# One more fill step between a chunk's layer norm and its transposes

## The chip, the cores and the metric

The kernel runs on one core of one Trainium2 chip. The metric is the device time of one execution in microseconds (us), as a median over runs. A core has five engines with queues of their own: PE (TensorE, matmuls and transposes; its weight loads appear as PEld), DVE (VectorE), ACT (ScalarE), POOL (GpSimd) and SP (SyncE, which here issues most DMAs). All data is fp32.

## The reference

The input x is a batch of two images of 128 channels and 64 x 64 places. Two layers are computed:

```
x = x + L0(group_norm(x))               # neighbourhood attention 7x7, 4 heads, and two small MLP steps
t = tokens of x                          # (2, 4096, 128)
q = layernorm(t)
t = t + softmax(q q^T / sqrt(128), diagonal masked) q
u = layernorm(t)
t = t + STU(u)                           # spectral filters (long causal convolutions, 16 of them, and
                                         # their sign-alternated twins), and a short part with 3 lags
out = tokens back to images
```

STU is summed over four branches with a one-hot weight, so that one branch counts. The layer norm of the line `u = layernorm(t)` and what turns u into the two inputs of STU are what the change touches.

## The kernel before, in words

**Stages.** Layer 0 runs first for both images, in an order written out by hand, up to about 350 us. Then come the attention of image 0, the attention of image 1, and the spectral convolution of both images with the output. The attention of image 0 covers leftovers of layer 0 and the preparation of image 1; the attention of image 1 covers leftovers of image 0 and the preparation of the filter matrices.

**Attention.** `attention(b, fill)` (L881) splits the 4096 tokens of image b into 8 chunks of 512, taken in the order CHUNKS = 0, 1, 4, 5, 2, 3, 6, 7. The scores are symmetric, so only the 36 pairs (a, c) with c at or after a are computed. A pair has four slots, numbered 0 to 3. In a slot PE computes the scores of a block of 128 tokens for the *next* pair (`weights`, L898, two half matmuls), ACT takes their exponential (L905), and PE applies the current pair's exponentials to the values: on a diagonal pair onto `own` (L926), else onto `other` (L951). On an off-diagonal pair, after slots 1 and 3, `turned` transposes blocks of exponentials (L912), DVE copies and sums them (L915), and one slot later they go onto `own` as well (L926). When a chunk has had its last contribution, `onto` calls `fill(CHUNKS[a], part)`, which puts a generator `after(b, c, part)` into the list `urgent`. This falls at the start of the next diagonal pair, in its slot 0. The last pair, (7, 7), has no next one, and so no `weights`.

**Filling.** At the end of each slot the loop calls `fill()` (L956), which advances one generator by one step: the first of `urgent` if there is one, else the first of `steps`. A generator that ends is dropped and the next one is asked. For image 0, `steps` holds the leftovers of layer 0 (`drain`), the branch weights, the filters' transform (`filters`, L1156) and the token norms of image 1 (`tokens`). For image 1 it holds what was left of image 0's `urgent` list, then `filter_matrices` (loads `st`, DVE sums L1107 to L1125) and `load_blocks`. `filler` (L1181) makes the pair of `fill` and `urgent`.

**After a chunk.** The steps of `after` (L968) are: transpose the chunk's attention output back to tokens (PE, L975) and divide and add the residual (DVE, L977 to L980); the layer norm into z (`layernorm`, L986: DVE statistics L170 and L171, DVE L160, POOL power L161, DVE L178); transpose z (PE, L989, which goes through the helper `transposed` and so shows as L189) and copy it to `zc` (ACT, L991); three steps with the segment transform of z (PE, L1011 twice and L1019), each with copies to `ub` (DVE and ACT, three buffers) and stores to `us` in HBM on SP's queue (L1000). After the fourth and the eighth chunk `short_lags` is appended, with eight steps (transposes of tt, L189 as well, and blocks of six half matmuls with `zc`, L1043, summed on DVE, L1050).

**The end of image 1.** The first `short_lags` of image 1 is kept back in `kept`. What is left in `urgent` after the attention of image 1 is run with one step of `kept` for each yield (L1259 to L1261). Then the convolution starts; its first loads (`ut`, L1287) reuse memory of image 1's tokens tt and read what was stored to `us`.

**Order.** PSUM banks for all this come from a ring of six (`bank`). In these stages the order in which the code emits instructions is a priority; the framework may place an instruction that is ready ahead of one emitted earlier on the same engine. In the convolution PE's order is the written one.

Of the kernel before, what the change touches and what calls it, by code (L numbers as in the profile page):

```python
# [93 lines left out]
def kernel(  # L94
# [87 lines left out]
    def layernorm(dst, src):  # L182

        ln_apply(dst, src, ln_statistics(src))

    def transposed(ps, src):

        for j in range(src.shape[1]):
            nc.tensor.transpose(ps[:, j * P : (j + 1) * P], src[:, j, :], ident)  # L189
# [667 lines left out]
    with ap_:  # L857
# [6 lines left out]
        def bank():  # L864
            return ps_m.tile([P, 512], F32, tag="bank", name="bank")
# [102 lines left out]
        def after(b, c, part):  # L968

            n0 = 4 * c  # L970
            ph, f0 = divmod(n0, FB)
            par, h = divmod(ph, 2)
            pt = bank()
            for j in range(4):
                nc.tensor.transpose(pt[:, j * P : (j + 1) * P], xa[b][:, (n0 + j) * P : (n0 + j + 1) * P], ident)  # L975
            rden = sp.tile([P, 4], F32, tag="rden", name="rden")
            nc.vector.tensor_reduce(rden, part[:, n0 : n0 + 4, :], AX.X, ALU.add)  # L977
            nc.vector.reciprocal(rden, rden)
            for j in range(4):
                nc.vector.scalar_tensor_tensor(  # L980
                    tt[b][:, n0 + j, :], pt[:, j * P : (j + 1) * P], rden[:, j : j + 1], tt[b][:, n0 + j, :],
                    ALU.mult, ALU.add,
                )
            yield
            z = sp.tile([P, 4, P], F32, tag="z4", name="z4")
            layernorm(z, tt[b][:, n0 : n0 + 4, :])  # L986
            yield
            pt = bank()
            transposed(pt, z)  # L989
            s0 = 1 + h * (TH // 2)  # L990
            nc.scalar.copy(  # L991
                zc[:, par, s0 : s0 + TH // 2].rearrange("p (c f) -> p f c", f=FB)[:, f0 : f0 + 4, :],
                pt.rearrange("p (f c) -> p f c", f=4),
            )
            yield
            z2 = z.rearrange("p f d -> p (f d)")

            def store(m0, q, src):
                mn = min(P, NC - m0)
                nc.sync.dma_start(  # L1000
                    out=us[m0 // 2 : (m0 + mn) // 2, :, 2 * h + q, f0 : f0 + 4, b, par, :].rearrange(
                        "g r f d -> (g r) f d"
                    ),
                    in_=src.rearrange("p (f d) -> p f d", d=P),
                )

            for m0 in (0, P):
                for q in range(2):
                    rows_ = slice(q * SB, (q + 1) * SB)
                    pu = bank()  # L1010
                    nc.tensor.matmul(pu, lhsT=tr[rows_, h, m0 : m0 + P], rhs=z2[rows_], start=True, stop=True)  # L1011
                    ub = sp.tile([P, 512], F32, tag="ub", name="ub", bufs=3)
                    (nc.scalar.copy if q else nc.vector.tensor_copy)(ub, pu)
                    store(m0, q, ub)
                yield
            pu = bank()
            for q in range(2):
                rows_ = slice(q * SB, (q + 1) * SB)
                nc.tensor.matmul(pu[rows_], lhsT=tr[rows_, h, 2 * P : NC], rhs=z2[rows_], start=True, stop=True)  # L1019
            ub = sp.tile([P, 512], F32, tag="ub", name="ub", bufs=3)  # L1020
            nc.scalar.copy(ub, pu)
            for q in range(2):
                store(2 * P, q, ub[q * SB : (q + 1) * SB])
            yield

        def short_lags(b, h):


            for par in range(2):
                n0 = (par * 2 + h) * FB  # L1030
                for f0 in range(0, FB, 4):
                    pt = bank()
                    transposed(pt, tt[b][:, n0 + f0 : n0 + f0 + 4, :])
                    nc.scalar.copy(xa[b][:, (n0 + f0) * P : (n0 + f0 + 4) * P], pt)
                    yield
                xv = xa[b][:, n0 * P : (n0 + FB) * P].rearrange("p (f c) -> p f c", f=FB)
                for c0 in range(0, P, 64):
                    py = bank()
                    for lag in range(3):
                        from_par = (par - lag) % 2  # L1040
                        back = (lag - par + from_par) // 2
                        s0 = 1 + (h * P + c0) * FB - back
                        nc.tensor.matmul(  # L1043
                            py, lhsT=mu[:, lag, :], rhs=zc[:, from_par, s0 : s0 + 512], start=(lag == 0), stop=(lag == 2)
                        )
                    pv = py.rearrange("p (c f) -> p f c", f=FB)
                    first = h == 0 and c0 == 0
                    for lo, hi, s in ((0, 32, 0), (32, 64, 1)) if first else ((0, 64, 2 + h),):
                        xs = xv[:, :, c0 + lo : c0 + hi]
                        nc.vector.scalar_tensor_tensor(  # L1050
                            xs, pv[:, :, lo:hi], seg[:, s : s + 1], xs, ALU.mult, ALU.add
                        )
                    yield
# [127 lines left out]
        def filler(b, steps, kept=None):  # L1181

            urgent, done = [], []

            def fill(c=None, part=None):
                if c is not None:
                    done.append(c)
                    urgent.append(after(b, c, part))
                    if len(done) % 4 == 0:
                        held = kept if kept is not None and len(done) == 4 else urgent  # L1190
                        held.append(short_lags(b, len(done) // 4 - 1))
                    return
                for queue in (urgent, steps):
                    while queue:
                        if next(queue[0], 0) is None:
                            return
                        queue.pop(0)

            return fill, urgent
# [294 lines left out]
```

## Time and profile before

| | |
|---|---|
| median of 3 runs | 2233.68 us (2232.13 to 2233.82) |
| the profiled execution | 2235.26 us |
| its span, first to last instruction | 2233.6 us |
| busy in the span: PE, PEld, DVE, ACT, POOL | 2165.4, 1333.8, 932.9, 783.4, 276.7 us |
| granted TensorE clock, mean | 0.991 |
| PE busy from 460 to 850 us | 383.58 of 390 |
| PE busy from 850 to 916 us | 62.08 of 66 |
| PE busy from 916 to 960 us | 44.00 of 44 |
| PE busy from 960 to 1290 us | 325.16 of 330 |
| PE busy from 1290 to 1330 us | 37.01 of 40 |

A row of the profile has a start, a duration, an engine, a line of the code, the operation with what it writes and reads, and how many instructions of that kind follow each other. A bracket at its end tells how long the engine stood idle before it and what released it. Matmuls are pipelined: they overlap on PE, so the distance between starts says more than durations. The five stretches of the table are the attention of image 0 from its first finished chunk, the first slots of image 1 with the leftovers of image 0, a stretch with attention alone, the rest of image 1, and the end of image 1 up to the convolution.

### The profile page before, as it was taken

The page shows a single profiled execution, that of the slowest core. Times are in us where ns is not written, and L with a number is a line of the kernel's source. Part 1 is how long each engine was busy: PE and PEld are TensorE (multiplying, and loading weights), DVE is VectorE, ACT ScalarE, POOL GpSimd, SP SyncE. Part 2 cuts the span into 40 slices and gives each one's busy share as a digit, 9 for nine tenths or more (in the row PEclk, how much of TensorE's full clock was granted, in tenths as well). Part 3 has the DMA queues.
Part 4 walks back from the last instruction along what each step waited for, and adds up shares of the span by engine and source line. Part 5 has one row for each costly group of instructions (what it writes and reads, how often), then busy time and mean ns, then how long its engine had stood idle before and what let it go on. Part 6 is the DMA issues. An engine that isn't in the chain of part 4 may idle for free.

```text
span 2233.6 us, 31536 instructions
## 1 busy us (share of the span) xinstructions
PE 2165.4 (97%) x11856; PEld 1333.8 (60%) x11856; DVE 932.9 (42%) x3038; ACT 783.4 (35%) x1904; POOL 276.7 (12%) x353
## 2 busy tenths in 40 slices
PE   5899998999999999999999999999999999999998
PEld 3577774544454444544544447677677777777766
DVE  4799985434443346433333342222213232323232
ACT  2789983222332223222222332322323232222232
POOL 3367874200000000000000000000000000000000
PEclk8999998999999999999999999999999999999999
DMA  4222222011000016100000122222222121212101
GB/s 110 72 62 61 61 55 51 1 57 62 24 24 22 8 44 181 38 24 15 10 24 24 47 82 68 50 48 59 47 51 59 39 59 39 59 39 59 40 10 76
DMA packets 174810, 109.53 MB, mean 49 GB/s; under 512 B 26049, under 2 KB 159809, under 8 KB 174146
## 3 DMA queue, kind: packets, MB, share of 16 engines
q1 hardware_dynamic: 171818, 105.24, 18.0%
q10 hardware_dynamic: 2840, 2.27, 0.4%
q8 instruction: 94, 1.54, 0.3%
q14 instruction: 58, 0.48, 0.1%
HBM read 72.87 MB, written 34.60 MB: 48 GB/s over the span
## 4 chain that ended last, share of the span: by engine, by line
PE 86%; DVE 6%; POOL 3%; DMA 2%; ACT 1%; issue 1%; SPq 1%; ACTq 0%; POOLq 0%; DVEq 0%
PE acc L1318 25%; PE pc L1306 13%; PE bank L898 10%; PE own L926 10%; PE other L951 8%; PE bank L912 4%; PE bank L332 2%; PE bank L189 2%; PE bank L542 2%; PE bank L1011 1%; PE bank L1043 1%; PE py L1340 1%; DMA st<-in_m_minus_dram 1%; PE po L564 1%; PE bank L506 1%
## 5 line engine op out<-in xcount | busy, mean ns | idle before, releaser
L1307 DVE COPY y<-pc 128x512 f32<-128x512 f32 x320 | 221.6, 692 | 351.5 <-PE pc L1306 347.8
L905 ACT ACTIVATE e<-bank 128x512 f32<-128x512 f32 x288 | 171.9, 597 | 552.5 <-PE bank L898 417.3
L898 PE MATMUL bank<-cm 128*128 128x512 f32 x576 | 298.9, 603 | 1.4 <-DVE y L653 1.4
L1318 PE MATMUL acc<-y,mpl 128*128 128x256 f32 x1280 | 292.1, 382 | 0.0
L1318 PE MATMUL acc<-y,mmi 128*128 128x256 f32 x1280 | 288.0, 379 | 0.0
L1306 PE MATMUL pc<-ct,ut 64*128 64x512 f32 x1280 | 285.2, 595 | 0.9 <-issue 0.9
L1318 PEld LDWEIGHTS acc<-y,mpl 128*128 128x128 f32 x1280 | 238.1, 190 | 59.4 <-issue 29.6
L1318 PEld LDWEIGHTS acc<-y,mmi 128*128 128x128 f32 x1280 | 242.6, 190 | 32.7
L1307 ACT COPY y<-pc 128x512 f32<-128x512 f32 x320 | 205.0, 641 | 86.5 <-PE pc L1306 86.5
L951 PE MATMUL other<-e,tok 128*128 128x512 f32 x448 | 228.6, 592 | 0.0
L926 PE MATMUL own<-et,tok 128*128 128x512 f32 x448 | 227.1, 594 | 1.4 <-DVE part L915 1.4
L915 DVE CUSTOM_DVE_ANT_0 et<-bank,one 128x512 f32<-128x512 f32 x224 | 145.7, 688 | 166.5 <-PE bank L912 166.3
L1306 PEld LDWEIGHTS pc<-ct,ut 64*128 64x128 f32 x1280 | 121.5, 187 | 145.8 <-issue 140.6
L1325 ACT COPY ob<-acc 128x256 f32<-128x256 f32 x32 | 19.3, 604 | 387.0 <-PE acc L1318 387.0
L926 PEld LDWEIGHTS own<-et,tok 128*128 128x128 f32 x448 | 84.4, 190 | 109.7 <-issue 72.6
L951 PEld LDWEIGHTS other<-e,tok 128*128 128x128 f32 x448 | 85.0, 190 | 106.6 <-issue 105.9
L898 PEld LDWEIGHTS bank<-cm 128*128 128x128 f32 x576 | 95.7, 193 | 73.8 <-issue 44.7
L1342 DVE TENSOR_TENSOR xa<-py,xa 128x512 f32<-128x512 f32 x32 | 22.1, 692 | 281.4 <-PE py L1340 281.4
L912 PEld LDWEIGHTS bank<-ident,e 128*128 128x128 f32 x896 | 103.3, 142 | 57.2 <-issue 43.6
L161 POOL TENSOR_TENSOR ln_rs<-ln_rs,mhalf 128x4 f32<-128x4 f32 x24 | 24.3, 1012 | 847.6 <-DVE ln_rs L160 847.6
L529 ACT ACTIVATE p<-p,mn 128x196 f32<-128x196 f32 x256 | 114.4, 449 | 22.2 <-DVE mn L519 14.0
L912 PE MATMUL bank<-ident,e 128*128 128x128 f32 x896 | 117.6, 274 | 0.0
(208 smaller groups left out, 2292.4 us busy)
## 6 DMA issues: line engine op xcount, KB each, us to landing
ut<-us SPq DMA_DIRECT2D x80, 256.0 KB
us<-ub SPq DMA_DIRECT2D x64, 256.0 KB
vw<-vd SPq DMA_DIRECT2D x256, 49.0 KB
ct<-gs SPq DMA_DIRECT2D x160, 72.0 KB
ct<-gs SPq DMA_DIRECT2D x160, 64.0 KB
gs<-sum SPq DMA_DIRECT2D x20, 256.0 KB
vd<-v SPq DMA_DIRECT2D x128, 32.0 KB
st<-in_m_plus_dram SPq DMA_DIRECT2D x16, 256.0 KB
```

The lines of the kernel that those rows point to most:

```text
L189: nc.tensor.transpose(ps[:, j * P : (j + 1) * P], src[:, j, :], ident)
L332: nc.tensor.matmul(pl, lhsT=wg[:, lo : lo + P], rhs=zT, start=True, stop=True)
L529: nc.scalar.activation(p, p, AF.Exp, bias=t[name + "mn"][:, h : h + 1], scale=-1.0, accum_out=t["den"][:, u, h : h + 1],)
L898: nc.tensor.matmul(ps, lhsT=cm[b][:, n * P : (n + 1) * P], rhs=cm[b][:, chunk(c)], start=True, stop=True)
L905: nc.scalar.activation(e, ps, AF.Exp, bias=0.0, scale=ASCALE, accum_out=part[:, n, c : c + 1])
L912: nc.tensor.transpose(pt[:, k * P : (k + 1) * P], es[k][:, m * P : (m + 1) * P], ident)
L915: nc.vector.tensor_tensor_reduce(et, pt, one, 1.0, 0.0, ALU.mult, ALU.add, part[:, n, a : a + 1])
L926: nc.tensor.matmul(own, lhsT=tok[b][:, n, :], rhs=e, start=first, stop=last)
L951: nc.tensor.matmul(other, lhsT=tok[b][:, 4 * CHUNKS[a] + j, :], rhs=es[j], start=(j == 0), stop=(j == 3))
L1306: nc.tensor.matmul(pc, lhsT=ut[fp, b, par, :], rhs=cv_[fp], start=True, stop=True)
L1307: (nc.scalar.copy if f else nc.vector.tensor_copy)(y[:, 4 * f : 4 * f + 4, :, par, b * 2 * FB + q : (b + 1) * 2 * FB : 2], pc.rearrange("p ...
L1318: nc.tensor.matmul(acc, lhsT=(mmi if l else mpl)[:, k, :], rhs=y[:, 1::2, k, ::-1, :] if l else y[:, 0::2, k, :, :], start=(l == 0 and k = ...
```

## The change

`after` yields twice between the norm and the transposes of z: once as before (None), and once with the value True. `fill` gives a True a meaning of its own: the generator has used its turn without work, so `fill` leaves the first list and takes a step of the next list, `steps`, if there is one. The generator stays where it is, and goes on with the transposes at the next call. A generator's end is now told by False instead of 0. Where `after` runs as part of `steps` (the leftovers of image 0 during image 1), the True ends the call without work; in the loop after the attention of image 1 it takes one more step of `kept`.

```diff
             z = sp.tile([P, 4, P], F32, tag="z4", name="z4")
             layernorm(z, tt[b][:, n0 : n0 + 4, :])
             yield
+            yield True
             pt = bank()
             transposed(pt, z)
             s0 = 1 + h * (TH // 2)
```

```diff
                         held.append(short_lags(b, len(done) // 4 - 1))
                     return
+
                 for queue in (urgent, steps):
                     while queue:
-                        if next(queue[0], 0) is None:
+                        got = next(queue[0], False)
+                        if got is None:
                             return
+                        if got:
+                            break
                         queue.pop(0)
```

## The prediction

> **What bounds the kernel now.** I read the page first. TensorE (PE) is busy for 97% of the span, and the chain that ended last is 86% PE. So an edit pays only where it removes time in which PE stands still, and it costs only where it makes PE stand still.
>
> ```profile
> PE 2165.4 (97%) x11856; PEld 1333.8 (60%) x11856; DVE 932.9 (42%) x3038; ACT 783.4 (35%) x1904; POOL 276.7 (12%) x353
> ```
>
> Next I read the view of waits for PE alone: engine and waiting line, what it waited for, total us, times, longest. Its first row is the step that the diff touches: the transposes of z (written at L189) wait for the norm's last instruction (L178).
>
> ```profile
> PE bank L189 <- DVE z L178: 14.5, 14, 3.2
> ```
>
> Then I looked at one of the fourteen in the order of PE's time (start, duration, line, what it writes and reads). L975 transposes the chunk, then come the norm's other engines, then z's transposes; L898 and L926 are attention.
>
> ```profile
> 709.75 0.60 PE L975 MATMUL bank<-ident,xa 128*128 128x128 f32 x4
> 710.18 1.02 PE L898 MATMUL bank<-cm 128*128 128x512 f32 x2
> 711.04 1.02 PE L926 MATMUL own<-e,tok 128*128 128x512 f32 x2
> 711.90 1.02 PE L898 MATMUL bank<-cm 128*128 128x512 f32 x2
> 712.76 1.02 PE L926 MATMUL own<-e,tok 128*128 128x512 f32 x2
> 714.52 0.75 PE L189 MATMUL bank<-ident,z 128*128 128x128 f32 x3 [0.74 <-DVE z L178]
> 715.11 1.02 PE L898 MATMUL bank<-cm 128*128 128x512 f32 x2
> 715.97 0.27 PE L189 MATMUL bank<-ident,z 128*128 128x128 f32 x1
> ```
>
> Starts tell more than the bracket. An attention pair starts every 0.86 us, so z could start at 712.76 + 0.86 = 713.62. It starts at 714.52, 0.90 late. Then the first three transposes come one by one as DVE delivers: L898 follows after 0.59 where four transposes otherwise take 0.43 (709.75 to 710.18). By the next transform (L1011 at 717.03) PE is behind an unbroken row (713.62 + 0.43 + 2 x 0.86 + 0.09 = 715.86) by 1.17 us. I use 1.17, not 0.74. The norm behind it, on DVE, with its one step on POOL (1.01 us, L161):
>
> ```profile
> 710.38 1.12 DVE L980 SCALAR_TENSOR_TENSOR tt<-bank,rden,tt 128x128 f32<-128x128 f32 x4 [1.66 <-PE bank L975]
> 712.67 0.17 DVE L160 TENSOR_SCALAR ln_rs<-ln_mv 128x4 f32<-128x4 f32 x1
> 714.03 1.11 DVE L178 TENSOR_SCALAR z<-tt,ln_mv,ln_rs 128x128 f32<-128x128 f32 x4 [1.19 <-POOL ln_rs L161]
> ```
>
> From L975's start to z's first transpose are 4.77 us; PE has 0.43 + 4 x 0.86 = 3.87 us of other work there. Eleven stalls have this shape (0.68 to 0.75): chunks 0, 1, 5, 2, 3 of image 0 and 0, 1, 4, 5, 2, 3 of image 1. Chunk 4 of image 0 shows no wait of PE itself, but starts slip by some 0.6. The others are two 1.60 stalls (chunk 6 of each image) and one of 3.21:
>
> ```profile
> 836.97 1.00 PE L189 MATMUL bank<-ident,z 128*128 128x128 f32 x4 [1.60 <-DVE z L178]
> 858.22 1.10 PE L189 MATMUL bank<-ident,z 128*128 128x128 f32 x4 [3.21 <-DVE z L178]
> ```
>
> [...] halves of 0.59 us start every 0.43. Hence the starts above. [...] at the 3.21 stall: DVE's filter sums wait for a load while the chunk's L980, whose transposes were issued at 850.11, stands behind them.
>
> ```profile
> 851.27 0.75 DVE L1109 SCALAR_TENSOR_TENSOR mmi<-st,wt,mmi 128x512 f32<-128x512 f32 x1 [1.07 <-DMA st<-in_m_minus_dram]
> 853.91 1.12 DVE L980 SCALAR_TENSOR_TENSOR tt<-bank,rden,tt 128x128 f32<-128x128 f32 x4
> ```
>
> **The change part by part.** No instruction is added or removed. A fill slot is one call of fill() in the attention loop. Now the slot after the norm belongs to `steps`, and z's transposes and the chunk's three transform steps come one slot later, with their stores (six DMAs a chunk, on SP's queue).
>
> 1. The extra slot as cover. Counting by the code, L975 falls in slot 0 of a diagonal pair's four, the norm in slot 1, the transposes in slot 2 before and 3 after: one more L898 and L926, 1.72 us. `steps` adds work only for chunks 0, 1, 4 of image 0 (filter sums, token norms) and chunk 0 of image 1 (a load); elsewhere it is empty, and attention alone is the cover. 3.87 + 1.72 = 5.59 us against 4.77: 0.8 to spare. All eleven go: 11 x 1.17 = 12.9 us. Chunk 4 of image 0: 0.6. Bounds by the bracket and by starts: 8.1 and 12.9; I take starts.
>
> 2. Chunk 6 of both images: its diagonal pair is the last, has no L898, and `steps` is empty. PE already runs all three remaining L926 pairs ahead of z (2.74 us from 832.63), so one slot later is the same place. 0.
>
> 3. Chunk 7 of image 0 runs in image 1's first slots, as part of `steps`. L975 comes one slot later (1.72), and between it and z there is 0.43 + 7 x 0.86 + 0.87 (eight transposes L912) = 7.3 us instead of 4.7. If DVE still begins L980 at 853.9, z comes at 858.2, that is 6.4 after the new L975: covered. By starts the stall cost 3.38 and about 0.7 behind it, 4.1 in all. But what is late next is known: from 838 to 911 the chain that ended last goes through the loads of the filter matrices, and PE's waits for L915 at 892.64 (0.56) and 911.14 (0.15) are bound by them through DVE's queue. PE arriving earlier waits longer there, unless those loads move up too. Bounds 0 and 4.1; I take 1.5.
>
> 4. The end of image 1. What is left after attention is mixed with the held short lags, one of theirs per yield. Before, chunk 7's norm lies under two short-lag blocks:
>
> ```profile
> 1301.42 0.60 PE L975 MATMUL bank<-ident,xa 128*128 128x128 f32 x4
> 1301.85 5.32 PE L1043 MATMUL bank<-zc,mu 128*128 128x512 f32 x12
> 1307.01 0.60 PE L189 MATMUL bank<-ident,z 128*128 128x128 f32 x4
> ```
>
> Chunk 6 leaves one step more, which uses up one short-lag block; chunk 7 then has L975, one block (2.58), two sets of transposes (0.43 each), z: 0.43 + 2.58 + 0.86 = 3.87 against 4.77. A new stall of 0.9 by the bracket's kind, 1.3 by starts; I take -1.1. Its stores come some 3 us later. Before, the transforms end at 1314.46 and SP has passed its stores by 1318.3; the first conv load is released at 1324.2 by the last tt transposes, not by stores. After, there lie 0.86 + 5.16 + 0.86 = 6.9 us from the last transform to the end of these transposes, and the stores need 3.9. Hidden, with 3.0 to spare; were that gone, each us would delay the conv stage by one.
>
> ```profile
> 1324.27 2.24 SPq L1287 DMA_DIRECT2D ut<-us  x5
> ```
>
> 5. The queues that the moved steps pass. The middle transform now comes directly ahead of L912, whose sums on DVE (L915) release L926. The DVE copy (0.69) can begin after half of the transform, before L912's first half is done: hidden; without that cover 0.69 per chunk. A store that holds up the next ub copy on ACT delays an exp that PE wants a pair later. Together with 838 to 911 I allow 1.4 for waits that I can't place (0 to 6).
>
> Sum: 12.9 + 0.6 + 0 + 1.5 - 1.1 - 1.4 = 12.5. The profiled execution took 2235.26 (span 2233.6 and 1.7 around it), 1.6 above the median shown: 2222.8 for such an execution, 2233.68 - 12.5 = 2221.2 for the median. I write 2221.5.
>
> **Rivals.** B: given back in part. The later transforms crowd the off-diagonal pairs, where L915's sums must be on time; 12 chunks x 0.69 = 8.3 back: about -5, 2229. For: 33.8 us of idle time ahead of L926's weight loads ends on L915's sums. Against: the loads overlap matmuls, and outside 838 to 911 PE waited for L915 only twice, 0.35 each.
>
> C: slower. DVE's queue between 838 and 911 holds 20.6 us of waits for the filter loads, most of them hidden now. If the changed order puts L915's sums behind them, PE pays. It decides above 12.4 us of that (12.9 + 0.6 - 1.1 is gained elsewhere), and is slower by a measurable amount above 16.9; all 20.6 would give +8, 2242. For: 3.21 us of such a wait already reached PE at 858. Against: since then they cost PE only 0.71.
>
> D: the change doesn't do what it says. The written order is a priority and instructions are placed by readiness (one L898 stands ahead of z's last transpose now). If z kept its place: 2233.7. Against: the added L898 and L926 now come ahead in the written order and wait for nothing new.
>
> **How the numbers follow.** The main case 0.70, B 0.14, C 0.09, D 0.07. The main case's own range is 2217 to 2226 (all of item 3: 2218.6, without the allowance a little less; the bracket's 8.1 in place of 12.9: 2226). To reach 8 in 10 I add most of B: 2215 to 2230. About 0.2%, 4.5 us, is what a measurement can tell from no change: faster 0.70 + 0.12 of B = 0.82; same 0.02 of B and 0.06 of D = 0.08; slower 0.10.
>
> **What would show it.** Right: the wait of L189 for z falls from 14.5 to about 4 (two 1.60, one new near the end of image 1); in the chunk shown, three L898 and three L926 between L975 and four z transposes in a row; PE's busy time unchanged; the conv stage starts some 12 us earlier, the same length. Wrong: PE's waits for L915 growing by more than 3 us; a conv start bound by us stores; chunk 6 losing its 1.60, which would make it better than I say.

## The result and the profile after

| | before | after |
|---|---|---|
| median | 2234.49 us (2232.13 to 2237.20) | 2224.14 us (2222.13 to 2226.11) |
| the profiled execution | 2235.26 us, span 2233.6 | 2222.13 us, span 2220.4 |
| first transposes (L975) of image 0's first chunk | 470.64 | 470.75 |
| first matmul of the convolution | 1330.24 | 1317.11 |
| from there to the end of the span | 903.3 | 903.3 |

After over before is 0.9951, 95% interval [0.9940, 0.9962]: faster by 10.3 us, or 0.5%. The predicted time was 2221.5 us, 2.6 us less, with a range of 2215 to 2230. Between the two profiled executions it is 13.13 us, all of it between the first two rows of times.

Lines after L988 have moved by one, those of the convolution by five: the segment transforms are L1012 and L1020 now, the short lags L1044 (PE) and L1051 (DVE), the filter sums L1108 to L1126. PE's line of the page:

```profile
PE 2159.5 (97%) x11856; PEld 1333.2 (60%) x11856; DVE 930.8 (42%) x3038; ACT 783.8 (35%) x1904; POOL 276.8 (12%) x353
```

The instructions are as many as before. In the view of PE's waits (total us, times, longest) the row that held 14.5 us in 14 stalls has three left, and a row that held 1.4 us has grown:

```profile
PE bank L189 <- DVE z L178: 5.0, 3, 2.0
PE own L926 <- DVE part L915: 4.2, 4, 2.9
```

The longest of the second row lies where the 3.21 for z was, in the first slots of image 1:

```profile
854.63 1.12 PE L926 MATMUL own<-et,tok 128*128 128x512 f32 x2 [2.90 <-DVE part L915]
```

PE's order in time, at the chunk that the prediction showed:

```profile
706.97 0.60 PE L975 MATMUL bank<-ident,xa 128*128 128x128 f32 x4
707.41 1.02 PE L898 MATMUL bank<-cm 128*128 128x512 f32 x2
708.27 1.02 PE L926 MATMUL own<-e,tok 128*128 128x512 f32 x2
709.12 1.02 PE L898 MATMUL bank<-cm 128*128 128x512 f32 x2
709.98 1.02 PE L926 MATMUL own<-e,tok 128*128 128x512 f32 x2
710.84 1.02 PE L898 MATMUL bank<-cm 128*128 128x512 f32 x2
711.70 1.02 PE L926 MATMUL own<-e,tok 128*128 128x512 f32 x2
712.56 0.60 PE L189 MATMUL bank<-ident,z 128*128 128x128 f32 x4
```

Three L898 and three L926 instead of two, no bracket, and four transposes of z in one row: from L975 to z are 5.59 us, each of them filled.

The distance between the L975 of successive chunks says what each step brought. Chunks are in their order 0, 1, 4, 5, 2, 3, 6, 7.

| part of the span | before minus after, us |
|---|---|
| the eleven chunks with stalls of 0.68 to 0.75 | 12.75 (1.10 to 1.18 each) |
| chunk 4 of image 0 | 0.62 |
| chunk 6 of image 0 to chunk 0 of image 1 (with chunk 7 of image 0) | 2.22 (130.03 to 127.81) |
| chunk 6 of image 1 to the convolution | -2.35 (38.54 to 40.89) |
| sum | 13.24; the start was 0.11 later: 13.13 |

### The profile page after: what moved, and what is told of

Same layout as the page of the kernel before. It is cut to its first block, busy times and chain, and to the rows that moved or that the text cites. A ratio compares the mean times of both kernels' runs of the same rounds, so it can differ in the third digit from the quotient of the medians.

```text
span 2220.4 us, 31534 instructions
## 1 busy us (share of the span) xinstructions
PE 2159.5 (97%) x11856; PEld 1333.2 (60%) x11856; DVE 930.8 (42%) x3038; ACT 783.8 (35%) x1904; POOL 276.8 (12%) x353
## 4 chain that ended last, share of the span: by engine, by line
PE 88%; DVE 4%; POOL 3%; DMA 2%; SPq 1%; ACT 1%; issue 1%; POOLq 0%; ACTq 0%; DVEq 0%
PE acc L1323 25%; PE pc L1311 13%; PE bank L898 11%; PE own L926 11%; PE other L951 8%; PE bank L912 4%; PE bank L332 2%; PE bank L1044 2%; PE bank L189 1%; PE bank L1012 1%; PE bank L542 1%; PE py L1345 1%; PE po L564 1%; PE bank L506 1%; ACT p L529 1%; POOL tok L703 1%
## 5 line engine op out<-in xcount | busy, mean ns | idle before, releaser
L898 PE MATMUL bank<-cm 128*128 128x512 f32 x576 | 298.7, 602 | 1.4 <-DVE y L653 1.4
L926 PE MATMUL own<-et,tok 128*128 128x512 f32 x448 | 227.4, 594 | 4.3 <-DVE part L915 4.2
L915 DVE CUSTOM_DVE_ANT_0 et<-bank,one 128x512 f32<-128x512 f32 x224 | 145.5, 687 | 133.8 <-PE bank L912 133.8
L926 PEld LDWEIGHTS own<-et,tok 128*128 128x128 f32 x448 | 84.2, 190 | 113.5 <-issue 72.6
L898 PEld LDWEIGHTS bank<-cm 128*128 128x128 f32 x576 | 94.8, 191 | 73.5 <-issue 49.4
L912 PEld LDWEIGHTS bank<-ident,e 128*128 128x128 f32 x896 | 103.0, 141 | 55.9 <-issue 48.6
L912 PE MATMUL bank<-ident,e 128*128 128x128 f32 x896 | 117.2, 274 | 0.0
```

The lines of the kernel that those rows point to most:

```text
L898: nc.tensor.matmul(ps, lhsT=cm[b][:, n * P : (n + 1) * P], rhs=cm[b][:, chunk(c)], start=True, stop=True)
L912: nc.tensor.transpose(pt[:, k * P : (k + 1) * P], es[k][:, m * P : (m + 1) * P], ident)
L915: nc.vector.tensor_tensor_reduce(et, pt, one, 1.0, 0.0, ALU.mult, ALU.add, part[:, n, a : a + 1])
L926: nc.tensor.matmul(own, lhsT=tok[b][:, n, :], rhs=e, start=first, stop=last)
```

## The experiments

My theory of the result: z's transposes waited for the latency of the norm's chain (DVE, POOL, DVE, 4.77 us), the attention matmuls of one more slot cover it, and it matters that they come between L975 and z. The rivals: other work that the True draws from `steps` is the cover; or what counts is that the later transforms come elsewhere.

**A slot with nothing drawn from `steps`.** Made from the kernel before: the added yield is a plain one, and `fill` is as it was.

```diff
             layernorm(z, tt[b][:, n0 : n0 + 4, :])
             yield
+            yield
```

> Edit: one more plain yield between the norm and z's transposes, and fill as it was: the extra slot does no other work. My theory (the slot's own attention matmuls, 1.72 us, are the cover): as the changed kernel, within 1.5 us of it, about 2224; PE's wait of L189 for z stays near 5 us, and each of the eleven chunks still gains 1.17 us by starts. Rival (the work put in the slot's place is needed as cover): the four chunks where the list of steps has work (0, 1, 4 of image 0 and 0 of image 1) lose their gain, 3 x 1.17 to 4 x 1.17, so 3.5 to 4.7 us above the changed kernel, and L189 waits for z there again.

Measured: 2227.11 us, ratio to before 0.9956 [0.9941, 0.9971], before's median on that chip 2235.37. By its time alone, 3.0 us above after, this run lies between theory and rival; the trace decides. The wait of L189 for z is 5.0 us, three times, as after. The chunk of the rows above has the same order (z 5.59 us after L975, no bracket), and ten of the eleven chunks gain what they gain after (eight transposes of `steps` come one chunk later here, in chunk 4's stretch instead of chunk 1's; that is taken into account). Chunk 0 of image 0 gains 0.13 only, with a new wait of 0.69 for L915 at 566.87 whose cause was not followed up. So the slot's own attention matmuls are the cover, and nothing drawn from `steps` is needed for it. The profiled execution took 2228.04, 5.9 more than after's, and most of it lies elsewhere: chunk 6 of image 0 to image 1 took 130.21 instead of 127.81, chunk 6 of image 1 to the convolution 44.11 instead of 40.89. In the latter stretch four matmuls of a transform (L1012, at 1286.72) took 2.08 us where the same four took 1.13 after (at 1283.58). The granted clock is 0.93 here from 845 to 870 us, 0.91 from 1270 to 1290 and 0.89 from 1290 to 1305, and 1.00 after in all three. That is worth about 5.2 us (an estimate: each stretch times what its clock lacks, 1.75 + 1.80 + 1.65). I come back to this below.

**The slot behind z's transposes.** The True stands one step later: z's transposes are where they were before, and only the transforms are moved.

```diff
-            yield True
             pt = bank()
             transposed(pt, z)
...
             yield
+            yield True
```

> Edit: the changed fill, but the extra yield stands behind z's transposes, ahead of the transforms. All later steps, their stores and the end of image 1 are moved as in the changed kernel; only the transposes stay where they were. My theory: no gain; L189 waits for z 14 us or more, as before; the end of image 1 loses 2 to 3 us because chunk 7's norm has less over it; about 2236. Rival (the gain comes from moving the transforms and stores away from the diagonal pair): about 2224, as the changed kernel.

Measured: 2239.67, ratio 1.0020 [1.0012, 1.0028]. The waits for z are all there, and grew:

```profile
PE bank L189 <- DVE z L178: 17.5, 15, 4.0
```

At the shown chunk it is 0.74 again. Moving the transforms and their stores alone gains nothing; it lost 4.3 us, more than the 1 or so that I expected, with 4.0 in place of 3.21 at chunk 7 of image 0, and 42.91 us from chunk 6 of image 1 to the convolution. So the second rival falls.

**A shorter chain, no slot.** The kernel before, whose norm after a chunk leaves out the power on POOL: the small constant is added to the variance on DVE, and that is used as it is. The output is another one.

```diff
-        rsqrt(rs[:, :n], mv[:, :n, 1], 1e-5)
+        if power:
+            rsqrt(rs[:, :n], mv[:, :n, 1], 1e-5)
+        else:
+            nc.vector.tensor_scalar(rs[:, :n], mv[:, :n, 1], 1e-5, None, ALU.add)
```

> Edit on the kernel before: the chunk's norm leaves out the power on POOL and scales by the variance itself; the computation is changed by that. No step is added. It takes 1.2 to 1.3 us out of the 4.77 between a chunk's transposes and z's. My theory (the stall is the norm's latency against 3.87 us of cover): the eleven stalls go without any move, 11 x 1.17 = 12.9 us, and the two of chunk 6 and the one of chunk 7 get about 1.2 shorter each, so 13 to 17 us below the kernel before, 2217 to 2221; L189's wait for z from 14.5 to under 3. Rival (moving the work matters, not the wait): within 2 us of the kernel before.

Measured: 2222.76, ratio 0.9938 [0.9922, 0.9955], 12.6 us below before. In its view of PE's waits (its lines are three further down):

```profile
PE bank L192 <- DVE z L181: 5.1, 3, 2.8
```

The eleven stalls are gone without any moved step; the rest is 1.13 at both chunks 6 and 2.80 at chunk 7 of image 0, which shrank by less than I expected. The eleven chunks gain 11.0 us in all, against 12.75 after. So it is latency against cover: one may shorten the one or lengthen the other, with nearly the same gain.

**The new stall at the end of image 1.** The kernel after, without the slot for the last two chunks of image 1.

```diff
-            yield True
+            if b == 0 or c < 6:
+                yield True
```

> Edit on the changed kernel: chunks 6 and 7 of image 1 skip the extra step, so that what is left after the last attention is run as before. My theory (the changed kernel loses 2.35 us there, because chunk 7's norm has one short-lag block less over it): the conv stage starts 2 to 2.5 us earlier than in the changed kernel, L189's last wait for z (1.95) is gone, and the time is about 2 below the changed kernel, 2222. Rival (the end of image 1 is late because of the stores, which the skip moves too, or because of what the earlier slots left): no difference over 0.5 us, or a new wait ahead of the conv stage.

Measured: 2221.53, ratio 0.9935 [0.9920, 0.9950]. From chunk 6 of image 1 to the convolution are 38.54 us, to the digit what the kernel before took; z of chunk 7 comes without a wait. So the whole of the 2.35 belongs to the slot at these two chunks.

**Fewer filter loads.** The kernel after, with the matrices of one branch loaded in place of four (the sums take that one four times over). The prediction named these loads as what makes L915 late at chunk 7 of image 0.

```diff
-                st = sp.tile([P, 4, P], F32, tag="st", name="st")
-                nc.sync.dma_start(out=st[:, 0:n], in_=src[i].rearrange("k d e -> d k e"))
+                if i == 0 or n < 4:
+                    st = sp.tile([P, 4, P], F32, tag="st", name="st")
+                    nc.sync.dma_start(out=st[:, 0:n], in_=src[i].rearrange("k d e -> d k e"))
```

> Edit on the changed kernel: the filter matrices load one block in four and use it for all four branches; the computation is changed by that, DVE's sums stay as many. My theory (PE's 2.90 and 0.55 for L915 in the first slots of image 1, which took the place of chunk 7's 3.21, come from DVE's queue waiting for filter loads): DVE's waits for st fall from 20 us to under 8, PE's wait for L915 from 4.2 to about 1, and from chunk 7's L975 to the next L975 are 105 to 106 us instead of 108.6; time 3 to 5 us below the changed kernel, about 2220. Rival (the sums L915 are late because the change put them behind the norm on DVE, whatever is ahead): L915 still over 2 us at that place, time within 1.5 us of the changed kernel.

Measured: 2225.28, ratio 0.9950 [0.9935, 0.9965]. The loads are out of the way (DVE's waits for them fall from some 20 us to 1.6) and PE waits nearly as long. DVE's order in time, from its one wait for a load to the norm of chunk 7 (four more sums, without a wait, are left out):

```profile
844.82 0.49 DVE L1109 TENSOR_SCALAR mpl<-st,wt 128x512 f32<-128x512 f32 x1 [1.60 <-DMA st<-in_m_plus_dram]
845.34 0.75 DVE L1111 SCALAR_TENSOR_TENSOR mpl<-st,wt,mpl 128x512 f32<-128x512 f32 x1
...
848.39 0.74 DVE L1111 SCALAR_TENSOR_TENSOR mmi<-st,wt,mmi 128x512 f32<-128x512 f32 x1
849.05 1.12 DVE L980 SCALAR_TENSOR_TENSOR tt<-bank,rden,tt 128x128 f32<-128x128 f32 x4
```

L980 could begin about 0.64 us after L975 (the distance in the kernel after at the chunk shown above, 706.97 to 707.61), which was at 844.05. It begins 4.4 us later than that, behind filter sums that mostly compute and don't wait. Behind L980 the whole norm and then L915 are late, and PE waited 2.58 for L915 at 853.26 (2.90 after). The later wait of 0.55 was gone. So my theory fell: not the loads, but the place of the filter sums in DVE's queue, ahead of a chunk's norm, makes this stall; with or without data to wait for. The loads do have a share further on. From chunk 6 of image 0 to image 1 took 127.56 us, hardly less than after's 127.81, but with a granted clock of 0.93 from 845 to 870 us, where after's is 1.00; at a full clock it would be some 125.8 (an estimate: 25 x 0.07 = 1.75 taken off).

**Two slots.** The kernel after, with a second True.

```diff
             yield True
+            yield True
```

> Edit on the changed kernel: two extra steps instead of one, for every chunk. My theory (one slot covers the eleven stalls with 0.8 us to spare): nothing more is gained at these eleven chunks, their distances stay within 0.2 us of the changed kernel's; chunk 6 of image 0 loses its 1.50 wait, because its transposes then come behind image 1's first scores; the end of image 1 is worse by 0 to 3 us. Time 2221 to 2226. Rival (distance itself gains, by letting the other engines run ahead): 1 us for each chunk again, 2214 or less.

Measured: 2218.00, ratio 0.9920 [0.9905, 0.9935], below the time that I expected: some 6 us below after by the medians, 4.0 by the profiled executions. Nothing more at the eleven chunks (chunk 2 to chunk 3 of image 0: 35.67, after 35.71), as expected of a stall that was already covered. Chunk 6 of image 0 loses its 1.50, but L926 waits 2.63 and 1.44 for L915 behind it, and the stretch to image 1 is only 0.36 shorter than after's. The end of image 1, which I expected to get worse, is the shortest so far (37.96): the norm of chunk 7 now lies under eight transposes and two short-lag blocks.

```profile
1290.07 0.60 PE L975 MATMUL bank<-ident,xa 128*128 128x128 f32 x4
1290.51 1.04 PE L189 MATMUL bank<-ident,tt 128*128 128x128 f32 x8
1291.38 5.32 PE L1045 MATMUL bank<-zc,mu 128*128 128x512 f32 x12
1296.53 0.60 PE L189 MATMUL bank<-ident,z 128*128 128x128 f32 x4
```

**One edit for each stall left.** The kernel after, without the slot for the last two chunks of image 1 and with two for chunk 6 of image 0.

```diff
-            yield True
+            for _ in range(2 if b == 0 and c == 6 else int(b == 0 or c < 6)):
+                yield True
```

> Edit on the changed kernel: no extra step for chunks 6 and 7 of image 1, two for chunk 6 of image 0, so that its transposes come behind the first scores of image 1. My theory: the wait of 1.50 for z at the start of image 1 goes (about 2 us by starts), the end of image 1 gains 2.35 as with the skip alone; about 2219.5, 4 to 5 below the changed kernel. Rival (what is saved at chunk 6 is waited for at L915 some us later, since DVE's queue is bound by the filter loads there): as the skip alone, 2221.5, with L915's wait up by 1.5 to 2.

Measured: 2223.09, ratio 0.9944 [0.9928, 0.9961]: 1.0 below after, not the 4 to 5 that I expected. The wait at chunk 6 of image 0 is gone (L189 waits for z once, 1.5), but the waits of L926 for L915 are 4.9 us in seven now, the longest 2.24. The rival was right in kind, but these waits grew by only 0.4 over the kernel with the skip alone (4.5 in four), and the stretch from chunk 6 of image 0 to image 1 is 1.1 shorter (128.61, there 129.71). In the profiled execution this is taken back at the end of image 1: 40.18 instead of 38.54, with matmuls at half their pace, as shown below.

**The filter sums behind chunk 7's norm.** The same kernel, but the sums take their branch weights from a tile `late` that a small DVE operation makes from the weights and from zeros times the copy of chunk 7's z. They can't be placed ahead of that copy any more. The whole computation is done.

```diff
+            late = tp.tile([P, NBR], F32, name="late")
+            nc.vector.scalar_tensor_tensor(
+                late, zc[:, 1, 1 + TH // 2 + 4 : 1 + TH // 2 + 8], 0.0, wt, ALU.mult, ALU.add
+            )
...
-                    mixed(dst[:, k0 : k0 + 4, :], src[:, k0 : k0 + 4])
+                    mixed(dst[:, k0 : k0 + 4, :], src[:, k0 : k0 + 4], late)
```

> Edit on the kernel with the skip and the two steps: one small DVE instruction more makes the weights of the filter sums depend on chunk 7's copy to zc in image 0, so that the filter sums (same loads, same count) begin behind its norm. Nothing is left out. My theory: DVE waits for st as long as before, but behind chunk 7; the 2.9 for L915 at chunk 7 goes and with it the slower clock behind it in some executions; 2 to 4 us below the kernel without this edit, about 2216.5. Rival (the waits only move): PE waits for L915 the same 3 us or more in the following pairs, time the same within 1.5 us or worse, since the sums then end later.

Measured: 2219.35, ratio 0.9926 [0.9911, 0.9940], 3.7 below the one without `late`, within the 2 to 4 that I expected. The two profiled executions took the same time (2220.33 and 2220.35), because the one with `late` came to image 0's first chunk 3.0 us later (471.89 against 468.90), ahead of anything that was edited; from chunk 6 of image 0 to image 1 it took 3.0 less (125.59 against 128.61). About 1.75 of that goes with the granted clock from 845 to 870 us, 0.93 without `late` and 1.00 with it (an estimate: 25 x 0.07). DVE's row for chunk 7, whose L975 was at 846.24:

```profile
846.87 1.13 DVE L980 SCALAR_TENSOR_TENSOR tt<-bank,rden,tt 128x128 f32<-128x128 f32 x4 [0.78 <-PE bank L975]
```

It starts 0.63 after L975, and the wait of 2.24 for L915 is gone (in all 3.1 us in six waits of 0.95 at most). Together with the run with few loads this shows that the order in DVE's queue was the cause of the stall at chunk 7.

**Both: two slots and the sums behind.**

```diff
             yield True
+            yield True
...
-                    mixed(dst[:, k0 : k0 + 4, :], src[:, k0 : k0 + 4])
+                    mixed(dst[:, k0 : k0 + 4, :], src[:, k0 : k0 + 4], late)
```

> Two extra slots at every chunk, and the filter sums made to depend on chunk 7's zc copy (a small DVE operation that adds zero times a piece of zc to the branch weights); the whole computation is done. My theory: the two edits act on different stalls. The second slot takes chunk 6's wait of 1.50 in image 0 and the short tail (first convolution matmul 37.96 after chunk 6's transposes, as with two slots alone); the dependence takes the wait of L915 at chunk 7 (2.63 there with two slots alone, about 0 here), so that no doubled spacing of matmuls shows between 845 and 870. Against two slots alone (2218.0) 1.5 to 3.5 less: 2214.5 to 2216.5. The rival: what one edit saves is waited again elsewhere, because with chunk 7 yet a slot later the filter sums themselves come late; L915's waits in total stay above 4 us and the time is 2218 or more.

Measured: 2212.14 us (2210.91 to 2214.21), ratio to before 0.9895 [0.9879, 0.9912]; before's median on that chip was 2235.43. The fastest of all: 23.3 us below before, 2.4 below what I expected at best. In PE's waits:

```profile
PE own L926 <- DVE part L915: 1.3, 4, 0.4
```

From chunk 6 of image 0 to image 1 are 122.52 us, against 127.45 with two slots alone, 125.59 in the run before this one, 127.81 after and 130.03 before: the two edits bring more together than apart, and no wait took the place of the ones removed. Against two slots alone about 1.75 of the 4.9 goes again with the granted clock from 845 to 870 us, 0.93 there and 1.00 here (an estimate, as above). The end of image 1 took 37.95. Of the waits for z one is left, 1.50 at chunk 6 of image 1.

**Matmuls at half their pace.** Two of these kernels run the same code at the end of image 1, with the same wait of 1.5 us before z of chunk 6. PE's order there: first the kernel without the slot for the last two chunks, then the one with one edit for each stall.

```profile
1283.79 1.09 PE L189 MATMUL bank<-ident,z 128*128 128x128 f32 x4 [1.51 <-DVE z L178]
1284.81 1.99 PE L1013 MATMUL bank<-z,tr 64*128 64x512 f32 x8
...
1288.82 0.60 PE L975 MATMUL bank<-ident,xa 128*128 128x128 f32 x4
```

```profile
1279.84 1.10 PE L189 MATMUL bank<-ident,z 128*128 128x128 f32 x4 [1.50 <-DVE z L178]
1280.87 3.39 PE L1013 MATMUL bank<-z,tr 64*128 64x512 f32 x8
...
1286.51 0.60 PE L975 MATMUL bank<-ident,xa 128*128 128x128 f32 x4
```

From z to the next L975 are 5.03 us in the one and 6.67 in the other, 1.64 more, with eight matmuls in 3.39 instead of 1.99. The granted clock from 1270 to 1290 us is 1.00 in the first and 0.91 in the second. The same happens around chunk 7 of image 0 (845 to 870 us), after the longest stall: clock 0.93 before (z's wait of 3.21), and 0.93 in the kernel without the slot at the end (L926's 3.1); but 1.00 after, in the execution that was profiled, with nearly the same wait of 2.90.

In before's trace the granted clock is 0.50 from 859.77 to 863.18 us, 1.55 us after the wait of 3.21 ended, and 1.00 before and behind that, from 450 to 2200 us. This costs about 1.7 us (an estimate: half of these 3.41 us), near the 1.64 above. In after's it is 1.00 from 450 to 2200 us. PE's longest wait at chunk 7 of image 0 and the granted clock from 845 to 870 us, in all eleven traces:

| kernel | longest wait, us | for | granted clock |
|---|---|---|---|
| before | 3.21 | z | 0.93 |
| after | 2.90 | L915 | 1.00 |
| slot with nothing drawn | 3.50 | L915 | 0.93 |
| slot behind z's transposes | 4.01 | z | 0.86 |
| shorter chain | 2.80 | z | 0.93 |
| no slot at the end | 3.05 | L915 | 0.93 |
| fewer filter loads | 2.58 | L915 | 0.93 |
| two slots | 2.63 | L915 | 0.93 |
| one edit for each stall | 2.24 | L915 | 0.93 |
| the same with `late` | 0.81 | L915 | 1.00 |
| both | none | | 1.00 |

At chunk 6 of image 1 eight traces have a wait of 1.50 or 1.51 for z between 1270 and 1290 us. The granted clock there is 0.91 in four of them (nothing drawn, fewer filter loads, one edit for each stall, the same with `late`) and 1.00 in the other four (after, no slot at the end, two slots, both). So the length of the wait does not settle it: 2.24 has the lower clock behind it, and 2.90 has not. What does settle it is not shown.

## Why the prediction was right

**Step 1, the extra slot as cover: right, in mechanism and size.** 12.75 us against 12.9, and 0.62 against 0.6 for chunk 4. The bracket's value, 8.1, would have been 4.7 too low; the starts held. (Starts were the right measure: half a matmul is recorded with 0.59 us in these traces and the next one starts 0.43 after it, so that durations overlap.) The empty slot shows that attention alone is the cover, the shorter chain that latency was the cause.

**Step 2, chunk 6: right.** A wait of 1.50 stays at both chunks; with two slots image 0's goes.

**Step 3, chunk 7 of image 0: the sign and the next wait right, the cause wrong, the size not settled by one trace.** As said, the 3.21 for z went and L926 waited for L915 in its place: 2.90 at once and 0.55 later. DVE at chunk 7 after, whose L975 was at 845.11:

```profile
845.52 0.75 DVE L1110 SCALAR_TENSOR_TENSOR mmi<-st,wt,mmi 128x512 f32<-128x512 f32 x1 [0.52 <-DMA st<-in_m_minus_dram]
...
848.75 0.28 DVE L1126 TENSOR_SCALAR mmi<-mdiff,sg 128x128 f32<-128x128 f32 x1
848.94 1.12 DVE L980 SCALAR_TENSOR_TENSOR tt<-bank,rden,tt 128x128 f32<-128x128 f32 x4
...
852.86 1.12 DVE L178 TENSOR_SCALAR z<-tt,ln_mv,ln_rs 128x128 f32<-128x128 f32 x4 [0.90 <-POOL ln_rs L161]
853.89 0.68 DVE L915 CUSTOM_DVE_ANT_0 et<-bank,one 128x512 f32<-128x512 f32 x1
```

From 845.52 to L980 DVE works without a wait. The norm begins 3.83 us after L975, as in the kernel before (3.80), where the prediction counted on 2.1 (853.9 less the new L975), and the sums for L926 stand behind it. The prediction blamed the filter loads; the few loads and `late` show that it is the order in DVE's queue, which PE's earlier arrival did not change here. With the allowance of step 5 the prediction had 0.1 for this part; the two executions differ by 2.22, but of these some 1.6 to 1.7 (an estimate: the 1.64 above, and half of 3.41) is the half pace that before's had from 859 to 864 (granted clock 0.50 from 859.77 to 863.18, L898 1.30 where 1.02 is usual, L1011 2.08 for 1.13, L912 1.45 for 1.09) and after's had not. The kernel without the slot at the end has the slot here too, and the half pace as well (granted clock 0.93 from 845 to 870 us, as before): 129.71 against 130.03, a gain of 0.3. So the slot itself brought some 0.3 to 0.6 here.

**Step 4, the end of image 1: right in sign, too small.** 2.35 lost where I took 1.1. The mis-sized term is the 4.77 us from L975 to z. PE after:

```profile
1288.91 0.60 PE L975 MATMUL bank<-ident,xa 128*128 128x128 f32 x4
1289.35 2.74 PE L1044 MATMUL bank<-zc,mu 128*128 128x512 f32 x6
1291.92 1.04 PE L189 MATMUL bank<-ident,tt 128*128 128x128 f32 x8
1294.91 0.30 PE L189 MATMUL bank<-ident,z 128*128 128x128 f32 x1 [1.95 <-DVE z L178]
```

The order and the cover of 3.87 are as worked out, but z comes 6.00 us after L975, since the sums of the short lags stand in DVE's queue, one pair ahead of L980 and one within the norm:

```profile
1289.18 0.88 DVE L1051 SCALAR_TENSOR_TENSOR xa<-bank,seg,xa 128x256 f32<-128x256 f32 x2 [3.75 <-PE bank L1044]
1289.98 1.11 DVE L980 SCALAR_TENSOR_TENSOR tt<-bank,rden,tt 128x128 f32<-128x128 f32 x4
...
1292.13 0.75 DVE L1051 SCALAR_TENSOR_TENSOR xa<-bank,seg,xa 128x512 f32<-128x512 f32 x1
```

L980 starts 1.07 after L975 instead of 0.64, and L178 4.44 after L980 instead of 3.64 (707.61 to 711.25 at the chunk shown first): 0.43 + 0.80 = 1.23, and 4.77 + 1.23 = 6.00. That the slot brings this loss is shown by the run without it; that the sums do is read from this order, and no run moved them. Both this and step 3 are the same omission: I counted what is queued behind a wait on DVE, but took the norm's own chain as if its queue were empty. That the stores are hidden was right: the convolution starts 7.08 us after the last tt transposes (1310.03 to 1317.11), as it did before (1323.16 to 1330.24).

**Step 5, the allowance of 1.4.** Away from chunk 7 of image 0 the waits for L915 are two of 0.35, as before, and nothing of the allowance was needed. At chunk 7 they are 3.45 us instead of 0.71, so that it belongs to step 3.

**The median.** The sum was made for the profiled execution, and there it is 13.13 against 12.5. That they lie so close is partly luck: 2.1 more than predicted at chunk 7, most of it before's half pace, stands against 1.25 less at the end of image 1. Without that half pace the difference would be about 11.4 (an estimate: 1.7 taken off). The medians differ by 10.35: after's profiled execution was the fastest of its six, 2.0 below their median, and before's was 0.8 above its own, and 13.13 - 2.0 - 0.8 = 10.3. Why after's others took longer is not shown, since only one execution of each kernel has a trace. Their times go with their mean granted clock: 2222.13 and 2223.05 at 0.992, 2224.18 and 2224.09 at 0.991, 2226.11 and 2225.89 at 0.990. Where in the span it was lower isn't shown for the executions without a trace. It is not full ahead of anything that the change touches either: from 0 to 400 us it is 0.96 before, after, with nothing drawn, without the slot at the end and with two slots, and 0.95 with both edits. The eleven traces come to image 0's first L975 between 468.90 and 471.89.

**The rivals.** B and C would have shown as L915 waits growing by 8 us or more; they grew by 2.8. D is refuted by PE's order at the chunk shown: z's transposes stand one L898 and one L926 later.

## What to carry to other kernels

Where an engine at 97% waits for a short chain on other engines, compare the chain's latency with the work that lies between its two ends in that engine's own order, by starts and not by idle brackets (1.17 instead of 0.74 here), and move the consumer one step of such work later. Before trusting the latency, read in the trace what else stands ahead of it on the engines that the chain passes: work of low priority that happened to be ready first (filter sums, short-lag sums) made the chain 1.2 us longer at the end of image 1 and 3.2 us at chunk 7 of image 0, just where the gain was lost. A dependence that holds such work back was worth 3.7 us by itself, part of it the half pace that went with the stall (about 1.75 between the two profiled executions, the estimate above), and with a longer cover the whole came to 23 us.

## What the runs showed that I had not expected

After some stalls of PE the matmuls of the next few us run at half pace, and after others of the same length they do not. At chunk 7 of image 0 eight of nine waits of 2.24 to 4.01 us went along with a granted clock of 0.93 or 0.86 from 845 to 870 us, and one of 2.90 with 1.00. At chunk 6 of image 1 four of eight waits of 1.5 us went along with 0.91 from 1270 to 1290 us, four with 1.00. Where the longest wait was 0.81 or there was none (the two kernels with `late`), the clock from 845 to 870 us was 1.00. So a stall of PE cost its own length in these runs and in some executions about 1.7 us besides (1.64 between the two kernels above; half of before's 3.41 us at 0.50 is 1.7, an estimate). What decides between the two was not shown. Whether a kernel without such stalls is also steadier was not shown: four runs of the fastest spread over 3.3 us, six of after over 4.0.
